# A fused decoder layer on one core: the cross-attention's output product of the first query tile, one slot later

## The chip, the cores and the metric

The kernel runs on one core of a Trainium2 chip. The metric is the device time of the program in microseconds (us): the median of the runs, beside one profiled execution, from which all spans, starts and durations come. Engines are named by what they do here: TensorE (PE in the profile, its weight loads PEld), VectorE (DVE), ScalarE (ACT), GpSimd (POOL) and SyncE (SP, which only issues DMAs here).

## The reference

A post-norm decoder layer over 32 entries of 256 tokens with 256 features, all in float32:

```python
x = _layernorm(x + self_attention(x))             # 16 heads of 64, 4 key/value heads, rotary, alibi
x = _layernorm(x + cross_attention(x, ctx, cell)) # 16 heads of 16, windows of 64 tokens
x = _layernorm(x + ffn(x))                        # 256 -> 1024 gate and up -> 256, quantised
```

The cross-attention normalises its attention output o once more before its output projection:

```python
return _proj(o, ln_o_w, ln_o_b, w_o, b_o)         # _ln(o) @ w_o.T + b_o
```

So for each tile of 128 query tokens: statistics of o, scaling, a product of 256 x 256, the residual, statistics of the sum, scaling. That is the part which the change touches.

## The kernel before, in words

The 256 tokens of an entry are two query tiles (t = 0 and 1) of 128. Everything is a software pipeline written out by hand at the end of `tile_decoder_kernel` (L870 to L945). Time is cut into steps, and each step into two slots (part 0 and part 1); an entry b owns the 16 slots from 16b. Each slot emits the fixed work of self-attention and cross-attention, and then advances the generators that are due in it. A generator (`self_inputs`, `cross_inputs`, `self_output`, `cross_output`, `feed_forward`) emits a piece of work and yields the number of slots until its next piece; a bare `yield` is one slot. TensorE, VectorE and ScalarE keep the order in which the instructions were emitted (L891); GpSimd and SyncE are given theirs by the framework. While entry b + 1 is in self-attention, entry b is in cross-attention and entry b - 1 in its feed-forward, so one slot mixes three entries.

In a slot of part 0 the order is: the inverse of the softmax sums (L433, L435), the exponentials of the second half of a cross unit (`cross_exp`, L684), the generators, then `self_turn` (the transposes t, L447, and their copies pT, L452), `cross_back` (xr, L729, and on VectorE L734 and L735), `cross_turn` (xt, L693, copy xpT, L695), a flush of the scalings that the generators left in the list `last` (L199), `self_scores` (s, L394; VectorE L410; ScalarE's exponentials L420), and every second step `self_values` (o, L464, copy oT, L471). In a slot of part 1 it is: `self_spread` (R, L479), `cross_exp`, the generators, `cross_values` (xo, L709, and its copy xoT, L718), `self_normal` (VectorE, L487), and again a flush.

`cross_output(b, t)` starts in slot 16b + 29 for t = 0 and in slot 16b + 37 for t = 1. Its pieces, one slot apart:
- statistics of o on VectorE (L178, L179) and their inverse root on GpSimd (`rstd_of`, L185 to L187);
- the scaling on ScalarE, through `last`;
- two transposes on TensorE into the bank zoT (L205) and ScalarE's copy to zT (L206);
- the product xw = zT times xo_w (L755, zT is what is loaded as weights), the residual sum on VectorE (L759), its statistics and inverse root (rstd_x);
- the scaling of the sum into x2 (L199).

For t = 0 the product falls into slot 16b + 32, a slot of part 0, and for t = 1 into slot 16b + 40. `feed_forward(b)`, which reads x2 of both tiles, starts in slot 16b + 42. In the slots 16b + 31 to 16b + 34 entry b - 1 is in its feed-forward: the up product (L802, L823), the maxima (L829 to L836), GpSimd's scaling L838 and VectorE's rounding L843. GpSimd also has the rotation of a query (L566 to L568), whose other half comes by two DMAs (L555) behind the eight kTz transfers (L640) on SyncE's queue.

All matmul outputs live in one pool of eight PSUM banks (L88), so a new output waits for the last reader of the bank that it is given. The buffers zT, xoT and x2 are doubled, xpT too.

Of the kernel before, what the change touches and what calls it, by code (L numbers as in the profile page):

```python
# [50 lines left out]
def kernel(  # L51
# [33 lines left out]
    def ctile(shape, dtype, name):  # L85
        return const.tile(shape, dtype, name=name, tag=name)
# [3 lines left out]
    def bank(name, shape=(P, 512), dtype=F32):  # L90
        return ps.tile(list(shape), dtype, tag="b", name=name)
# [12 lines left out]
    def work(name, shape, bufs=2, dtype=F32):  # L104
        return sb.tile(list(shape), dtype, tag=name, name=name, bufs=bufs)
# [50 lines left out]
    for i in range(2):  # L156


        t = ctile([P, (NT + 1) * XH * XE + 32 - XE], F32, f"xvaug{i}")
# [14 lines left out]
    def stats(src, name):  # L174

        st = small("st", 6)
        mv = small(f"mv_{name}", 2)
        nc.vector.bn_stats(st, src)  # L178
        nc.vector.bn_aggr(mv, st)  # L179
        return mv  # L180

    def rstd_of(mv, name):

        rb = small(f"rstd_{name}", 2)
        nc.gpsimd.tensor_scalar(rb[:, 0:1], mv[:, 1:2], EPS, None, ALU.add)  # L185
        nc.gpsimd.tensor_tensor(rb[:, 0:1], rb[:, 0:1], neg_half[:, 0:1], ALU.pow)
        nc.gpsimd.tensor_scalar(rb[:, 1:2], mv[:, 0:1], rb[:, 0:1], -1.0, ALU.mult, ALU.mult)  # L187
        return rb
# [12 lines left out]
    def transposed(dst, src, name):  # L201

        pt = bank(name)
        for dc in range(NDC):
            nc.tensor.transpose(pt[:, dc * P : (dc + 1) * P], src[:, dc * P : (dc + 1) * P], ident)  # L205
        nc.scalar.copy(dst, pt[:, 0 : NDC * P].rearrange("p (c t) -> p c t", t=P))  # L206
# [535 lines left out]
    def cross_output(b, t):  # L742
        s = state[b]
        on = s["on", t]
        mv = stats(on, "zo")
        rstd = rstd_of(mv, "zo")
        yield
        last.append(partial(scaled, on, on, rstd))
        yield
        zoT = work("zT", [P, NDC, P])  # L750
        transposed(zoT, on, "zoT")
        yield
        py = bank("xw")
        for dc in range(NDC):
            nc.tensor.matmul(py[:, 0:D], zoT[:, dc, :], xo_w[:, dc, :], start=(dc == 0), stop=(dc == NDC - 1))  # L755
        if t == 0:
            s["x2"] = work("x2", [P, NT, D])
        h = s["x2"][:, t, :]
        nc.vector.tensor_tensor(h, py[:, 0:D], s["x1", t], ALU.add)  # L759
        mv = stats(h, "x2")  # L760
        rstd = rstd_of(mv, "x2")
        yield
        last.append(partial(scaled, h, h, rstd))
# [117 lines left out]
    for b in range(B):  # L881
        s0 = 16 * b
        if b:
            at(s0 - 16, self_inputs(b))
        at(s0 + 2, cross_inputs(b))
        for t in range(NT):
            at(s0 + 2 * (5 + 4 * t), self_output(b, t))
            at(s0 + 2 * (CROSS + 5 + 4 * t) + 1, cross_output(b, t))
        at(s0 + 2 * (CROSS + 11) + 2, feed_forward(b))
# [145 lines left out]
```

## Time and profile before

| what | value |
|---|---|
| median of 3 runs | 2324.79 us (2323.94 to 2325.04) |
| the profiled execution, its own time | 2327.47 us |
| its span, first to last instruction | 2325.7 us |
| mean granted TensorE clock | 0.987 |
| VectorE / ScalarE / GpSimd busy | 1701.3 / 1764.8 / 1124.2 us |
| steady stretch 250 to 2090 us: TensorE busy | 1827.02 of 1840 us |
| first 250 us: TensorE busy | 227.22 of 250 us |
| from 2090 us on: TensorE busy | 192.68 of 235.7 us |
| one entry, from one first-tile product to the next (913.37 to 983.02) | 69.65 us |

How to read it: a busy share is an average over the span. The ends of TensorE's matmuls are modelled, so the starts of two groups that follow each other tell more than a printed duration. A line in order of time has the start, the duration, engine and line, what is written from what, the shape and the count; in brackets stands how long the engine was idle before it and what ended that.

### The profile page before, as it was taken

The numbers are of one execution on the slowest core, as the hardware profiler recorded it, in microseconds if no ns is written. First come the engines' busy times: TensorE is split into PE (matmuls) and PEld (weight loads), VectorE is DVE, ScalarE is ACT, GpSimd is POOL, SyncE is SP. The second block draws the span as 40 slices with busy tenths as digits, with TensorE's granted clock in tenths as the row PEclk, the third lists the DMA queues.
The fourth block names the chain that finished last, engine by engine and source line by source line (L and its number), as shares of the span: only waits on it lengthen the run. The fifth ranks groups of instructions, "written<-read, shape, count | busy, mean of one in ns | idle before, by whom it ended". The sixth has DMA issues, their size and how long they took to land.

```text
span 2325.7 us, 54754 instructions
## 1 busy us (share of the span) xinstructions
PE 2246.9 (97%) x17637; PEld 1689.2 (73%) x17700; DVE 1701.3 (73%) x6949; ACT 1764.8 (76%) x5057; POOL 1124.2 (48%) x1851
## 2 busy tenths in 40 slices
PE   7999999999999999999999999999999999999985
PEld 5677777777777777777777777777777777777652
DVE  3767777777777777777777777777777777777765
ACT  2677777878777878777878777878777878777873
POOL 5344545445545545545445545445545444545432
PEclk9999999999999999999999999999999999999996
DMA  6311211112211111211111211112211111211000
GB/s 211 87 51 47 58 53 49 47 45 52 59 52 49 47 45 53 57 51 49 47 47 54 56 51 49 47 46 54 56 51 50 46 48 53 55 47 44 20 22 10
DMA packets 105407, 123.05 MB, mean 53 GB/s; under 512 B 21792, under 2 KB 74912, under 8 KB 105120
## 3 DMA queue, kind: packets, MB, share of 16 engines
q1 hardware_dynamic: 103424, 115.96, 18.7%
q10 hardware_dynamic: 1696, 3.57, 0.4%
q8 instruction: 142, 2.33, 0.4%
q14 instruction: 145, 1.19, 0.2%
HBM read 39.50 MB, written 8.39 MB: 21 GB/s over the span
## 4 chain that ended last, share of the span: by engine, by line
PE 78%; DVE 10%; ACT 8%; issue 1%; POOL 1%; DMA 1%; SPq 0%; ACTq 0%; POOLq 0%; DVEq 0%
PE proj L331 12%; PE s L394 10%; PE wo L495 10%; PE t L447 8%; PE o L464 8%; PE xt L693 4%; ACT p L420 4%; PE xs L655 4%; DVE gu L817 3%; PE xw L755 3%; PE xv L616 3%; PE ffo L855 3%; DVE p L410 2%; PE R L479 2%; PE xk L604 2%; PE v L363 2%
## 5 line engine op out<-in xcount | busy, mean ns | idle before, releaser
L420 ACT ACTIVATE p<-p,nm 128x256 f32<-128x256 f32 x1024 | 508.0, 498 | 168.6 <-DVE nm L410 164.7
L410 DVE CUSTOM_DVE_ANT_0 p<-s,alibi 128x256 f32<-128x256 f32 x1024 | 372.7, 420 | 180.5 <-PE s L394 180.4
L452 ACT COPY pT<-t 128x512 f32<-128x512 f32 x512 | 275.2, 591 | 127.1 <-PE t L447 126.8
L684 ACT ACTIVATE xp<-xp,xnm 128x128 f32<-128x128 f32 x1024 | 326.1, 394 | 5.9 <-DVE xnm L668 5.9
L394 PE MATMUL s<-kT,qT 64*128 64x256 f32 x2048 | 290.8, 402 | 0.0
L447 PE MATMUL t<-ident,p 128*128 128x128 f32 x2048 | 269.0, 273 | 3.2 <-ACT p L420 3.2
L447 PEld LDWEIGHTS t<-ident,p 128*128 128x128 f32 x2048 | 237.9, 141 | 31.4 <-ACT p L420 6.6
L331 PE MATMUL proj<-xT,wq_sb 128*128 128x256 f32 x1024 | 251.8, 389 | 0.0
L464 PE MATMUL o<-pT,v 128*64 128x256 f32 x2048 | 250.0, 385 | 0.0
L495 PE MATMUL wo<-wo_sb,oT 128*128 128x256 f32 x1024 | 245.3, 382 | 0.0
L668 DVE CUSTOM_DVE_ANT_0 xp<-xs,mask 128x128 f32<-128x128 f32 x1024 | 225.9, 286 | 2.9 <-PE xs L655 2.1
L495 PEld LDWEIGHTS wo<-wo_sb,oT 128*128 128x128 f32 x1024 | 189.4, 190 | 47.4 <-issue 22.7
L355 POOL TENSOR_TENSOR qT<-qT,other 128x512 f32<-128x512 f32 x128 | 162.9, 1273 | 120.6 <-DMA other<-psin 53.3
L394 PEld LDWEIGHTS s<-kT,qT 64*128 64x128 f32 x2048 | 176.5, 186 | 54.7 <-issue 23.5
L340 DVE TENSOR_TENSOR psin<-proj,rs_sb 128x512 f32<-128x512 f32 x160 | 110.2, 689 | 141.7 <-PE proj L331 141.7
L331 PEld LDWEIGHTS proj<-xT,wq_sb 128*128 128x128 f32 x1024 | 186.4, 191 | 32.8 <-issue 6.4
L464 PEld LDWEIGHTS o<-pT,v 128*64 128x64 f32 x2048 | 135.7, 136 | 98.3 <-issue 22.9
L420 ACT ACTIVATION_READ_ACCUMULATOR p<-p,nm 128x1 f32 x1024 | 192.6, 188 | 0.0
L695 ACT COPY xpT<-xt 128x512 f32<-128x512 f32 x256 | 153.2, 598 | 6.1 <-PE xt L693 4.2
L693 PE MATMUL xt<-ident,xp 128*128 128x128 f32 x1024 | 154.2, 274 | 0.0
L655 PE MATMUL xs<-kTz,xqT 64*64 64x512 f32 (+1 forms) x768 | 136.6, 611 | 5.0 <-POOL xqT L568 5.0
L817 DVE SCALAR_TENSOR_TENSOR gu<-gu,ff 128x512 f32<-128x512 f32 x128 | 82.3, 682 | 72.8 <-ACT gu L816 72.8
(156 smaller groups left out, 4528.2 us busy)
## 6 DMA issues: line engine op xcount, KB each, us to landing
other<-psin SPq DMA_DIRECT2D x640, 64.0 KB, 2.0
xT<-in_xt_dram SPq DMA_DIRECT2D x32, 256.0 KB, 2.7
xs<-in_x_dram SPq DMA_DIRECT2D x32, 256.0 KB, 2.7
cs<-in_ctx_dram SPq DMA_DIRECT2D x32, 256.0 KB, 2.7
other<-qb SPq DMA_DIRECT2D x64, 128.0 KB, 2.0
kTz<-tr SPq DMA_DIRECT2D x256, 32.0 KB, 2.0
other<-qb SPq DMA_DIRECT2D x128, 64.0 KB, 1.9
out_dram<-x SPq DMA_DIRECT2D x32, 256.0 KB, 2.2
```

Of the source, the lines that this page charges most:

```text
L331: nc.tensor.matmul(pq[:, c * L : (c + 1) * L], w[:, dc, c * P : (c + 1) * P], xT[:, dc, :], start=(dc == 0), stop=(dc == NDC - 1),)
L394: nc.tensor.matmul(banks[half][:, rr * L : (rr + 1) * L], qT[rows_, rr, qc * P : (qc + 1) * P], kT[rows_, kc, :], start=(rr == 0), stop=(r ...
L410: nc.vector.tensor_tensor_reduce(p[:, cols], banks[half][:, cols], alibi[:, 2 * (4 * kc + 2 * rp + rr) + half, :], -0.125, 3.0e38, ALU.add ...
L420: nc.scalar.activation(p[:, cols], p[:, cols], AF.Exp, bias=nm[:, rr : rr + 1], scale=-1.0, accum_out=s["sums", i // 2][:, (2 * rp + rr) * ...
L447: nc.tensor.transpose(pt[:, j * P : (j + 1) * P], p[half][:, rr * L + kk * P : rr * L + (kk + 1) * P], ident,)
L452: nc.scalar.copy(pT[half], pt)
L464: nc.tensor.matmul(po[half * HD : (half + 1) * HD, rp * L : (rp + 1) * L], s["v"][:, kk, (2 * kc + half) * HD : (2 * kc + half + 1) * HD], ...
L495: nc.tensor.matmul(py[:, 0:D], s["oT", qc, kc][:, r, :], wo_sb[:, 4 * kc + r, :], start=(kc == 0 and r == 0), stop=(kc == 1 and r == 3),)
L655: nc.tensor.matmul(banks[half].rearrange("p (h k) -> p h k", k=P)[q0:q1], s["xqT", qc][rows_, ch, q0:q1], kTz[rows_, ch, :, k0 : k0 + P], ...
L668: nc.vector.tensor_tensor_reduce(p[:, cols], banks[half][:, cols], s["mask"][:, qc, :], -1.0, 3.0e38, ALU.add, ALU.min, s["xnm", i][half][ ...
L684: nc.scalar.activation(p[:, cols], p[:, cols], AF.Exp, bias=s["xnm", i][half][:, j : j + 1], scale=-1.0)
L693: nc.tensor.transpose(pt[:, j * P : (j + 1) * P], p[:, j * P : (j + 1) * P], ident)
```

## The change

One yield in `cross_output` now counts two slots for the first query tile, and one as before for the second:

```diff
         zoT = work("zT", [P, NDC, P])
         transposed(zoT, on, "zoT")
-        yield
+        yield 1 + (t == 0)
         py = bank("xw")
         for dc in range(NDC):
             nc.tensor.matmul(py[:, 0:D], zoT[:, dc, :], xo_w[:, dc, :], start=(dc == 0), stop=(dc == NDC - 1))
```

So for t = 0 the product and all behind it (the sum, its statistics, the inverse root, the scaling) come one slot later: the product in slot 16b + 33 and the scaling in slot 16b + 34. On TensorE the product then stands behind t, xr, xt, s, o and R, and ahead of wo (L495). On VectorE L759, L178 and L179 stand behind the four score operations L410 and behind L836, ahead of L487. On GpSimd rstd_x stands behind the rotation L566 to L568, in most entries between the two L838. On ScalarE the scaling stands behind the copies pT and xpT of the next slot and ahead of its exponentials. The PSUM banks are handed out in the new order, so t, xr, xt, s, o, R and wo of that stretch get other banks than before. No operation is added or taken away, and no DMA is moved.

## The prediction

> **What bounds the kernel now.** I read the page's busy rows and slices first, then the chain that ended last, then TensorE's waits (cut to the steady stretch, 250 to 2090 us), then one entry's turn in order of time, engine by engine.
>
> ```profile
> PE 2246.9 (97%) x17637; PEld 1689.2 (73%) x17700; DVE 1701.3 (73%) x6949; ACT 1764.8 (76%) x5057; POOL 1124.2 (48%) x1851
> PEclk9999999999999999999999999999999999999996
> PE 78%; DVE 10%; ACT 8%; issue 1%; POOL 1%; DMA 1%; SPq 0%; ACTq 0%; POOLq 0%; DVEq 0%
> ```
>
> TensorE is busy for 97% of the span at full clock and carries 78% of the chain. So only what TensorE waits for, or what its stream contains, is worth anything. Its waits in the steady stretch are a single line (columns: who waited, for whom; us in total, times, longest):
>
> ```profile
> PE xw L755 <- ACT zT L206: 10.2, 26, 0.4
> ```
>
> That is the product this change moves, waiting for ScalarE's copy of the transposed tile. Over the whole run it is 17.4 us in 34 waits: 31 are the first query tile of entries 0 to 30, three belong to the drain at the end. The second tile's product never waits in the steady state. One entry (TensorE, then ScalarE, in order of time; start, duration, then the group):
>
> ```profile
> 911.94 1.04 PE L802 MATMUL ff<-ff_up,xiT 128*128 128x512 bf16 x3
> 913.37 1.13 PE L755 MATMUL xw<-xo_w,zT 128*128 128x256 f32 x4 [0.40 <-ACT zT L206]
> 914.34 1.04 PE L447 MATMUL t<-ident,p 128*128 128x128 f32 x8
> 915.21 0.38 PE L729 MATMUL xr<-ident,xoT 128*128 128x128 f32 x2
> ```
>
> ```profile
> 912.97 0.35 ACT L206 COPY zT<-zoT 128x256 f32<-128x256 f32 x1
> 913.22 0.37 ACT L718 COPY xoT<-xo 128x256 f32<-128x256 f32 x1
> 913.48 1.29 ACT L684 ACTIVATE xp<-xp,xnm 128x128 f32<-128x128 f32 x4
> 915.03 1.07 ACT L452 COPY pT<-t 128x512 f32<-128x512 f32 x2 [0.26 <-PE t L447]
> ```
>
> The same product for the second tile, where nothing is late, gives the undisturbed pace:
>
> ```profile
> 947.13 1.03 PE L755 MATMUL xw<-xo_w,zT 128*128 128x256 f32 x4
> 947.99 1.04 PE L447 MATMUL t<-ident,p 128*128 128x128 f32 x8
> 948.87 0.38 PE L729 MATMUL xr<-ident,xoT 128*128 128x128 f32 x2
> ```
>
> **What the stall really costs.** The 0.40 us shown is counted from a modelled matmul end, so I use starts. Undisturbed, the four records of the product take 947.99 - 947.13 = 0.86 us, and the eight transposes 0.88 us. The four records of the feed-forward group (one is missing) also take 0.86, so the product was due at 911.94 + 0.86 = 912.80 and came at 913.37: 0.57 late. It then took 914.34 - 913.37 = 0.97 instead of 0.86, because its own weights (zT is the stationary operand) could not be loaded ahead: another 0.11. The stall is 0.68 us per entry.
>
> **What is late next.** With the product gone from this place, the transposes t start at 912.80; their exponentials were finished at 911.39 (ScalarE's order of time), and the PSUM banks that the changed program gives them were read last by VectorE at 911.85 and by ScalarE's bias at 913.06 (needed by the second group's weight load at about 913.13: just in time). The transposes end at 912.80 + 0.88 = 913.68, and next is xr, whose weights are xoT. ScalarE writes that right after zT: 913.22 + 0.37 = 913.59, plus the 0.05 that passed between zT's end (913.32) and the product (913.37) = 913.64, plus 0.11 for a weight load that wasn't ahead = 913.75. So a small wait of about 0.07 remains. In before, xr came at 915.21; less the 0.86 of product that moves behind it, 914.35. Gain per entry: 914.35 - 913.75 = **0.60 us**. The bounds: 0.68 if xoT makes no wait, and nothing if a later wait eats it all.
>
> **Parts that cost nothing, and their cover.**
> The product itself: the same four records, in the next slot between R and wo. Its bank was freed by a copy of pT some 2 us earlier and zT has been ready for over 4 us; TensorE pays 0.86 there as it did here.
> VectorE: the sum and statistics (L759, L178, L179: 0.42 + 0.43 + 0.18, about 1.0 us) leave the queue ahead of xr's normalisation and the self scores, where VectorE had 0.79 us of idleness waiting for s, and enter behind the feed-forward's L836, ahead of L487. L836 ended at 920.54 and would end near 919.1 (the scores start 0.60 + 0.86 = 1.46 us earlier); the product, behind R, is done at about 919.0; L487 then ends near 920.9, and VectorE stood waiting until 921.68 anyway for GpSimd (the lines are GpSimd's, VectorE's and ScalarE's):
>
> ```profile
> 920.52 1.13 POOL L838 TENSOR_SCALAR gu<-gu,ffhup 128x1024 f32<-128x1024 f32 x1
> 921.68 0.69 DVE L843 TENSOR_SCALAR gu<-gu 128x1024 bf16<-128x1024 f32 x1 [0.54 <-POOL gu L838]
> 924.75 0.51 ACT L420 ACTIVATE p<-p,nm 128x256 f32<-128x256 f32 x1 [1.37 <-DVE nm L410]
> ```
>
> So 0.8 us of cover. If it were gone, L487, L843 and the next scores behind L759 would be late.
> GpSimd: rstd_x (0.22 + 0.57 + 0.27, with gaps 1.26 us) moves from ahead of the rotation L566 to 568 behind the first L838. L566 started at 918.28 on a DMA that SyncE issued only after eight kTz transfers, so the rotation, the first L838 and L843 stay where they are in time. The second L838 waits for VectorE until 924.29, behind which 1.26 us fit.
> ScalarE: the scaling L199 (0.60) moves into the next slot, ahead of four exponentials. They wait 1.37 us for VectorE there; rstd_x comes at 922.9 to 923.5, so L199 ends by 924.1. It hides, with 0.6 to spare. SyncE's queue keeps its order; the change issues no DMA.
> Semaphore waits: the first t now waits for three engines, which needs one or two more wait instructions of 0.051 us on TensorE's sequencer, at most 0.1 x 31 = 3 us. The t of the next slot already has two waits and starts on its pace; I take zero.
>
> **A rule that speaks against it.** L843 used to start with GpSimd idle; now rstd_x stands ready behind L838. The Trainium skill (SBUF — State Buffer, "Who interferes with whom") says that GpSimd and a VectorE copy or tensor_scalar in a two-port mode take one pair of ports in turn, each for its whole instruction. One place of this trace has just that, with another GpSimd operation queued behind L838:
>
> ```profile
> 2238.50 1.20 DVE L843 TENSOR_SCALAR gu<-gu 128x1024 bf16<-128x1024 f32 x1 [0.19 <-POOL gu L838]
> 2238.43 0.73 POOL L566 TENSOR_TENSOR qb<-qb,rx_sb 128x256 f32<-128x256 f32 x1
> 2239.12 1.18 POOL L567 TENSOR_TENSOR other<-other,rx_sb 128x256 f32<-128x256 f32 x1
> ```
>
> L843 lost 0.51 (1.20 against 0.69) to the one operation that was ahead, and then went before the next. By that row L843 loses what is left of the first rstd operation, 0.15 to 0.22 us. By the rule read at its worst (all three first) it loses 1.26. What follows L843 is VectorE's chain to the scores, ScalarE's exponentials (924.75) and at last the copies of pT, which TensorE's group o needs. Those copies ran from 930.23 to 931.30 against a need, after the 0.60 shift, at 931.89 - 0.60 + 0.70 = 931.99: 0.64 us of slack, with 0.05 for the semaphore. A delay of 0.2 costs nothing; 1.26 costs 0.62 per entry and with it the gain.
>
> **Sum.** 31 entries x 0.60 = 18.6 us. The last entry's product does not wait (its ScalarE is ahead), and in the drain the move shifts about 1 us of VectorE work by a slot: taken as zero, within 0.5 either way. The profiled execution took 2327.47 us (span 2325.7): it would be 2308.9. The median of the runs is 2324.79, 2.7 below that execution: **2306.2**.
>
> **Rivals.**
> 1. Part of the gain is eaten. L843 loses two GpSimd operations (0.22 + 0.57 + a gap of 0.08 = 0.87): 0.87 - 0.64 = 0.23 per entry at o, 7 us: 2313. Or ScalarE's xoT comes 0.3 later than now: 9 us, 2315. For it: ScalarE is in one run from 904 to 913 with hardly a gap. Against it: the offsets of zT and xoT to the product are the same within 0.01 us in all 31 entries. Chance 0.20.
> 2. The wait merely moves to xr, xt or o, so that the kernel doesn't do what the move says: 2324. That would need ScalarE to be the bound from slot to slot, but it waited 0.26 for t at 915.03 and 0.94 for the scores after that. Chance 0.05.
> 3. Slower: rstd_x becomes late and, at the head of ScalarE's queue, L199 holds back the exponentials behind it. It decides from 1.24 us of delay of these (0.64 slack + 0.60 gain), which is rstd_x at 925.4, 2 us after my estimate. At 925.75 it costs 0.31 x 31 = 10 us: 2334. Against it: the rotation ahead of it is held by the SyncE queue to a fixed time. Chance 0.05.
>
> **How the numbers follow.** The main case is 2303.8 (0.68 per entry) to 2309.5 (0.1 per entry for waits and semaphores): 0.68; a little more gain 0.02. The range goes on to 2314 to take in the first half of rival 1. A measurement of this kernel tells 0.2% (4.6 us) from no change, so everything below 2320.1 is faster: 0.68 + 0.02 + 0.20 = 0.90; the same 0.05; slower 0.05.
>
> **What would show it.** After: no wait of xw on zT in the steady stretch; t following the feed-forward's group at once; xr with a wait of 0.0 to 0.1 us on xoT; the period of an entry 69.65 (913.37 to 983.02) less 0.60; the scores' first VectorE operation 1.5 us earlier relative to the feed-forward; L843 at 0.7 to 0.9 us, and L199 of the first tile between xpT and the exponentials with no wait behind it. I'd be wrong if TensorE shows a new wait of over 0.3 us at xr or at o, or if ScalarE's exponentials of the next slot wait for L199.

## The result and the profile after

| kernel | median us | runs | range |
|---|---|---|---|
| before | 2324.91 | 6 | 2323.94 to 2326.14 |
| changed | 2305.03 | 6 | 2303.58 to 2307.11 |

The ratio is 0.9916, with a 95% interval of 0.9903 to 0.9928: 19.9 us less. The forecast was 2306.2. The profiled execution of the changed kernel took 2305.13 us, its span 2303.3.

The same rows of the page as were shown of before, now of the changed kernel:

```profile
PE 2244.9 (97%) x17700; PEld 1692.6 (73%) x17700; DVE 1697.7 (74%) x6949; ACT 1757.6 (76%) x5057; POOL 1137.0 (49%) x1851
PE 93%; DVE 3%; ACT 2%; POOL 1%; DMA 1%; issue 1%; SPq 0%; POOLq 0%; DVEq 0%; ACTq 0%
```

TensorE's busy time is what it was (2246.9 before); the span shrank around it. The chain that ended last now lies on TensorE for 93% instead of 78%: it no longer leaves TensorE for VectorE and ScalarE once an entry in order to reach zT. In the steady stretch the table of TensorE's waits is empty. The busy time of the same 1820 us (stretch, its length, then TensorE's busy time and records, granted clock, DMA share, GB/s), of before:

```profile
250.00:2070.00 1820.00, 1807.07 (x14364) 1.00 0.19 51
```

and of the changed kernel:

```profile
250.00:2070.00 1820.00, 1820.00 (x14538) 1.00 0.20 51
```

By the modelled ends of its matmuls TensorE has not one gap left there. One entry of the changed kernel on TensorE, in order of time:

```profile
905.66 1.04 PE L802 MATMUL ff<-ff_up,xiT 128*128 128x512 bf16 x4
906.54 1.04 PE L447 MATMUL t<-ident,p 128*128 128x128 f32 x8
907.41 0.39 PE L729 MATMUL xr<-ident,xoT 128*128 128x128 f32 x2
907.64 0.60 PE L693 MATMUL xt<-ident,xp 128*128 128x128 f32 x4
...
911.11 0.66 PE L479 MATMUL R<-ident,wide 128*128 128x128 f32 x4
911.60 1.03 PE L755 MATMUL xw<-xo_w,zT 128*128 128x256 f32 x4
912.47 1.89 PE L495 MATMUL wo<-wo_sb,oT 128*128 128x256 f32 x8
```

and the two copies on ScalarE that it used to wait for:

```profile
906.68 0.36 ACT L206 COPY zT<-zoT 128x256 f32<-128x256 f32 x1
906.94 0.37 ACT L718 COPY xoT<-xo 128x256 f32<-128x256 f32 x1
```

The transposes t follow the feed-forward's group at once (0.88 us from start to start), xr follows t after 0.87, and the product, now 4.56 us behind the end of zT, takes 912.47 - 911.60 = 0.87. The next entry's product starts at 980.61, so an entry takes 980.61 - 911.60 = 69.01 us. Before it took 69.65. That is 0.64 to 0.65 us an entry, and 31 x 0.65 = 20 us, the whole difference.

### The profile page after: what moved, and what is told of

Same layout as the page of the kernel before. It is cut to its first block, busy times and chain, and to the rows that moved or that the text cites. A ratio compares the mean times of both kernels' runs of the same rounds, so it can differ in the third digit from the quotient of the medians.

```text
span 2303.3 us, 54792 instructions
## 1 busy us (share of the span) xinstructions
PE 2244.9 (97%) x17700; PEld 1692.6 (73%) x17700; DVE 1697.7 (74%) x6949; ACT 1757.6 (76%) x5057; POOL 1137.0 (49%) x1851
## 4 chain that ended last, share of the span: by engine, by line
PE 93%; DVE 3%; ACT 2%; POOL 1%; DMA 1%; issue 1%; SPq 0%; POOLq 0%; DVEq 0%; ACTq 0%
PE proj L331 12%; PE s L394 11%; PE o L464 10%; PE wo L495 9%; PE t L447 9%; PE xs L655 5%; PE ff L802 5%; PE xt L693 5%; PE R L479 3%; PE xo L709 3%; PE xv L616 3%; PE ffo L855 3%; PE xw L755 2%; PE xq L532 2%; PE xk L604 2%; PE v L363 2%
## 5 line engine op out<-in xcount | busy, mean ns | idle before, releaser
L410 DVE CUSTOM_DVE_ANT_0 p<-s,alibi 128x256 f32<-128x256 f32 x1024 | 372.5, 420 | 161.6 <-PE s L394 161.2
L495 PE MATMUL wo<-wo_sb,oT 128*128 128x256 f32 x1024 | 245.2, 382 | 0.0
L495 PEld LDWEIGHTS wo<-wo_sb,oT 128*128 128x128 f32 x1024 | 191.8, 190 | 49.0 <-issue 23.5
L566 POOL TENSOR_TENSOR qb<-qb,rx_sb 128x256 f32<-128x256 f32 (+1 forms) x96 | 87.6, 913 | 125.7 <-DMA other<-qb 76.5
```

The lines of the kernel that those rows point to most:

```text
L410: nc.vector.tensor_tensor_reduce(p[:, cols], banks[half][:, cols], alibi[:, 2 * (4 * kc + 2 * rp + rr) + half, :], -0.125, 3.0e38, ALU.add ...
L495: nc.tensor.matmul(py[:, 0:D], s["oT", qc, kc][:, r, :], wo_sb[:, 4 * kc + r, :], start=(kc == 0 and r == 0), stop=(kc == 1 and r == 3),)
```

## The experiments

Each ratio is to the kernel before, run on the same chip, with its 95% interval. A period is the mean time from one entry's key projection (L604) to the next one's, over 25 entries, from the starts in the trace; it is 69.66 us before and 69.00 in the changed kernel.

| run | median us | ratio to before | period us |
|---|---|---|---|
| product in its old slot, a ready operand | 2306.34 | 0.9919 [0.9905, 0.9933] | 69.00 |
| product in its old slot, the rest a slot later | 2325.13 | 1.0002 [0.9993, 1.001] | 69.65 |
| product two slots later | 2332.72 | 1.0033 [1.002, 1.0045] | 69.82 |
| changed, one ScalarE step ahead of xoT | 2307.15 | 0.9922 [0.991, 0.9935] | 69.09 |
| changed, only the scaling a slot later | 2306.29 | 0.9923 [0.9911, 0.9935] | 69.02 |
| changed, more VectorE work ahead of the scores | 2312.29 | 0.9946 [0.9934, 0.9959] | 69.20 |
| changed, two GpSimd powers more | 2305.29 | 0.9918 [0.9905, 0.9932] | 69.01 |
| changed, four GpSimd powers more | 2307.87 | 0.9927 [0.9914, 0.9941] | 69.03 |
| changed, five ScalarE steps ahead of xoT | 2319.03 | 0.9976 [0.9966, 0.9986] | 69.47 |
| changed, a chain of eight GpSimd additions | 2323.16 | 0.9991 [0.9983, 0.9999] | 69.42 |

### The wait alone, without the move

```diff
+            lhs = zoT[:, dc, :] if t else xo_w[:, dc, 0:P]
-            nc.tensor.matmul(py[:, 0:D], zoT[:, dc, :], xo_w[:, dc, :], start=(dc == 0), stop=(dc == NDC - 1))
+            nc.tensor.matmul(py[:, 0:D], lhs, xo_w[:, dc, :], start=(dc == 0), stop=(dc == NDC - 1))
```

> The kernel before, with its order kept: the product of the first query tile stays in its slot, but takes a block of the weights xo_w as its stationary operand in place of zT, so it has nothing to wait for (zT is still made, and not read; the cross-attention's output of the first tile is therefore something else). Theory (the gain is the wait on zT and nothing else): TensorE's wait at L755 is gone in the steady stretch, 0.66 us an entry, x 31 = 20.5, so 2304 to 2305, as fast as the changed kernel. Rival (the gain comes of the new order on VectorE, ScalarE and the PSUM banks, the wait only being where it showed): most of it stays away, 2315 to 2325, and a wait shows at the next product or transposes.

Measured: 2306.34, and the period of the changed kernel to the hundredth. The order of the kernel before costs nothing by itself; its wait on zT is the whole of the 20 us. The rival, a gain through the new order, is out.

### Everything but the product moved

```diff
             nc.tensor.matmul(py[:, 0:D], zoT[:, dc, :], xo_w[:, dc, :], start=(dc == 0), stop=(dc == NDC - 1))
+        if t == 0:
+            yield
```

> The kernel before with the product in its old slot, but all behind it (the sum and its statistics on VectorE, the inverse root on GpSimd, the scaling on ScalarE) one slot later, as in the changed kernel. Theory: the wait on zT stays, 2324 to 2326, although VectorE's scores start earlier. Rival (the gain is VectorE's and ScalarE's new order): 2305 to 2312.

Measured: 2325.13, no change. TensorE's waits of this run in the stretch from 250 to 2070 us (who waited, for whom; us, times, longest):

```profile
PE xw L755 <- ACT zT L206: 10.1, 26, 0.4
```

The row is that of before within 0.1 us. VectorE's earlier scores bring nothing as long as TensorE stands still.

### The product two slots later

```diff
-        yield 1 + (t == 0)
+        yield 1 + 2 * (t == 0)
```

> The changed kernel with the first tile's product two slots later than before in place of one, ahead of the transposes of the next step. Theory: any place works where zT is ready and the sum is in time for the feed-forward: 2304 to 2306, TensorE without a wait at the product. Rival (the place one slot later is special, because the work behind the product hides there): VectorE's sum now stands ahead of the scores of a slot whose exponentials follow VectorE at once, so 2310 or more.

Measured: 2332.72, slower than before the change: my theory as it stood there fell. TensorE's order is that of the changed kernel, group by group (R, xw, wo, t), because no fixed TensorE work stands between these two places. What moved is VectorE's sum and statistics, and ScalarE's scaling. In order of time, TensorE of this run:

```profile
918.13 1.03 PE L755 MATMUL xw<-xo_w,zT 128*128 128x256 f32 x4
919.00 1.89 PE L495 MATMUL wo<-wo_sb,oT 128*128 128x256 f32 x8
...
930.43 1.13 PE L394 MATMUL s<-kT,qT 64*128 64x256 f32 x8
932.10 2.47 PE L464 MATMUL o<-pT,v 128*64 128x256 f32 x16 [0.54 <-ACT hiT L851]
934.50 0.66 PE L479 MATMUL R<-ident,wide 128*128 128x128 f32 x4
```

VectorE's, where the sum stands directly ahead of the scores of the next step:

```profile
924.48 0.41 DVE L759 TENSOR_TENSOR x<-xw,x 128x256 f32<-128x256 f32 x1
924.92 0.43 DVE L178 BATCH_NORM_STATS2 st<-x 128x6 f32<-128x256 f32 x1
925.38 0.18 DVE L179 BATCH_NORM_AGGREGATE mv_x<-st 128x2 f32<-128x6 f32 x1
925.48 0.39 DVE L410 CUSTOM_DVE_ANT_0 p<-s,alibi 128x256 f32<-128x256 f32 x1
```

and, of SyncE, TensorE and ScalarE, the eight kTz transfers, the scores two slots ahead of o and the copy hiT:

```profile
909.68 6.13 SPq L640 DMA_DIRECT2D kTz<-tr  x8
922.13 1.13 PE L394 MATMUL s<-kT,qT 64*128 64x256 f32 x8
931.06 0.99 ACT L851 COPY hiT<-hiT 128x1024 bf16<-128x1024 bf16 x1
```

The same three of the changed kernel:

```profile
903.15 5.75 SPq L640 DMA_DIRECT2D kTz<-tr  x8
915.60 1.13 PE L394 MATMUL s<-kT,qT 64*128 64x256 f32 x8
922.66 0.99 ACT L851 COPY hiT<-hiT 128x1024 bf16<-128x1024 bf16 x1
```

The product doesn't wait, but o does. Undisturbed, o follows s after 1.06 us and R follows o after 1.88 (909.23 - 908.17 and 911.11 - 909.23 in the changed kernel). Here it is 1.67 and 2.40, so in this entry o lost 0.61 + 0.52 = 1.13 us: first, by the releaser that the line names, to ScalarE's copy hiT, then to the copies pT behind it. ScalarE's copy hiT started 931.06 - 922.13 = 8.93 us after the start of s two slots earlier. In the changed kernel it was 922.66 - 915.60 = 7.06. So ScalarE came 1.87 us late and TensorE lost 1.13: a slack of 0.74 us. VectorE's 1.0 us and the scaling's 0.5, now between xoT and the exponentials of the second half, explain 1.5 of the 1.87. The rest came by SyncE's queue: the eight kTz transfers, whose issue began 12.45 us ahead of s in both, kept it for 6.13 us here and for 5.75 there, and the DMAs L555 behind them, GpSimd's rotation L566, its scaling L838 and VectorE's L843 all came 0.4 later behind them.

This start differs from entry to entry; why SyncE's queue takes longer in one than in another stays open. Over 25 entries of this run TensorE lost 0.12 to 2.08 us, 0.82 in the mean by the period. Read over 25 entries each of the changed kernel and of the runs built on it, o loses nothing as long as hiT starts no more than 7.79 us behind s, and about the excess from there on (0.04 us at 7.83, 0.11 at 7.90, 0.19 at 7.98). For the entry shown of the changed kernel that is a slack of 7.79 - 7.06 = 0.73 us. In its other entries hiT starts 6.42 to 7.72 us behind s, so the slack lies between 0.07 and 1.37. The entry with the least of it (GpSimd, TensorE, ScalarE):

```profile
1326.30 0.73 POOL L566 TENSOR_TENSOR qb<-qb,rx_sb 128x256 f32<-128x256 f32 x1 [2.75 <-DMA other<-qb]
1329.61 1.14 PE L394 MATMUL s<-kT,qT 64*128 64x256 f32 x8
1337.33 0.99 ACT L851 COPY hiT<-hiT 128x1024 bf16<-128x1024 bf16 x1
```

### How close xr stands

```diff
+        if i == 2:
+            nc.scalar.copy(small("step", 1), neg_half[:, 0:1])
         nc.scalar.copy(oT, po[:, 0 : 2 * P])
```

> The changed kernel with one more small ScalarE copy (128 x 1, some 0.2 us with its start) in front of the copy to xoT in the slot ahead of the transposes xr, once an entry. Theory (after the change TensorE reaches xr with no slack: xoT's end sets it within 0.05 us): each 0.2 us shows in full, 31 x 0.2 = 6 us, 2311, with a wait at xr on xoT. Rival (there is slack at xr): 2305.

Measured: 2307.15, 2.1 us more than the changed kernel and not 6; by the intervals alone that is not clear of none. The periods tell more: 0.09 us an entry. The step's record lasts 0.20 us, but xoT started only 0.10 after it: I had taken the record's length for the price, although the Trainium skill (ScalarE: Activation LUTs, "What ACT_TABLE_LOAD costs") says that activations one behind the other overlap by some 93 ns, which fits 0.20 - 0.10 here, where the operations are copies. Five steps make the dose clear:

```diff
         if i == 2:
-            nc.scalar.copy(small("step", 1), neg_half[:, 0:1])
+            for _ in range(5):
+                nc.scalar.copy(small("step", 1), neg_half[:, 0:1])
```

> The changed kernel with five small ScalarE copies in front of the copy to xoT in place of one. One of them moved xoT by 0.10 us (from start to start), so five move it by 0.5. Theory (TensorE reaches xr with no slack, and a wait there costs its length): xr comes 0.5 to 0.6 us later in each entry, 16 to 19 us, 2321 to 2324, so nearly the whole gain is gone and the wait stands at xr on xoT. Rival (ScalarE takes it up, since it waits for TensorE at the next copies anyway): under 2312.

Measured: 2319.03, 14 us of the 20 given back. ScalarE of that run:

```profile
910.99 0.56 ACT L720 COPY step<-neg_half 128x1 f32<-128x1 f32 x5
911.45 0.37 ACT L721 COPY xoT<-xo 128x256 f32<-128x256 f32 x1
```

TensorE:

```profile
910.59 1.04 PE L447 MATMUL t<-ident,p 128*128 128x128 f32 x8
911.87 0.44 PE L732 MATMUL xr<-ident,xoT 128*128 128x128 f32 x2 [0.25 <-ACT xoT L721]
912.15 0.60 PE L693 MATMUL xt<-ident,xp 128*128 128x128 f32 x4
```

xoT moved by 911.45 - 910.99 = 0.46 us and the period by 69.47 - 69.00 = 0.47: one for one, a little under the 0.5 to 0.6 expected. There is no slack at xr; the changed kernel arrives there just when xoT does.

### The scaling's place, and VectorE's

```diff
         rstd = rstd_of(mv, "x2")
-        yield
+        yield 1 + (t == 0)
         last.append(partial(scaled, h, h, rstd))
```

> The changed kernel with only ScalarE's scaling L199 of the first tile one more slot later, so that it stands behind xoT and ahead of the second half's exponentials, as it does in the run with the product two slots later. It puts 0.5 us into ScalarE's stretch ahead of the copies hiT and pT, which TensorE's group o waits for. In the run two slots later that stretch came 1.87 us later relative to TensorE than in the changed kernel and o waited 1.13, so the slack is 0.74 us. Theory (one stretch with 0.74 us of slack): 0.5 is hidden, 2304 to 2306. Rival (the scaling's new place is what cost the time there): 0.5 x 31 = 15 us, 2320.

Measured: 2306.29, period 69.02. The 0.5 us on ScalarE are hidden, as the slack says, but for four of 25 entries whose slack was smaller than that: they lost 0.04 to 0.27 us.

```diff
         yield
+        if t == 0:
+            for _ in range(3):
+                nc.vector.bn_stats(small("more", 6), wo_sb[:, 0, :])
         last.append(partial(scaled, h, h, rstd))
```

> The changed kernel with three more VectorE statistics of a constant (0.45 us each from start to start, 1.35 in all) once an entry, right ahead of the scores two slots behind the product's old place; nothing reads them. Theory: 1.35 less 0.74 of slack shows at o, 0.61 x 31 = 19 us, 2324. Rival (VectorE's place doesn't matter, ScalarE's does): 2305.

Measured: 2312.29, 7 us more and not 19. The dose was smaller than I had reckoned: from VectorE's order of time of this run,

```profile
920.70 1.07 DVE L765 BATCH_NORM_STATS2 more<-wo_sb 128x6 f32<-128x256 f32 x3
921.68 0.41 DVE L410 CUSTOM_DVE_ANT_0 p<-s,alibi 128x256 f32<-128x256 f32 x1
```

the three took 0.98 us together (they depend on nothing, and run 0.33 apart), and hiT came 926.78 - 918.82 = 7.96 us after s, 0.90 late. TensorE at o in this entry:

```profile
928.18 2.11 PE L464 MATMUL o<-pT,v 128*64 128x256 f32 x16
930.23 0.65 PE L479 MATMUL R<-ident,wide 128*128 128x128 f32 x4
```

o took 2.05 instead of 1.88, a loss of 0.17, so the slack is again 0.73. Over 25 entries the loss ran from nothing to 0.89 us, and the period grew by 0.20. The mechanism held, and the size of the dose was wrong.

### A late inverse root

```diff
         mv = stats(h, "x2")
+        if t == 0:
+            late = small("late", 1)
+            for _ in range(2):
+                nc.gpsimd.tensor_tensor(late, mv[:, 1:2], neg_half[:, 0:1], ALU.pow)
```

> The changed kernel with two more GpSimd powers (0.57 us each, 1.3 with their gaps) ahead of the first tile's inverse root, once an entry; nothing reads them. The inverse root is then ready 1.3 us later, ScalarE's scaling L199 waits for it, and the exponentials behind L199, which had 0.64 us to spare, start some 0.6 later. Theory (0.74 us of slack at o): nothing of it shows, 2304 to 2307. Rival (the third one of the prediction: a late inverse root at the head of ScalarE's queue decides): 0.6 x 31 = 19 us, 2324.

Measured: 2305.29. GpSimd and ScalarE of this run:

```profile
908.89 0.73 POOL L566 TENSOR_TENSOR qb<-qb,rx_sb 128x256 f32<-128x256 f32 x1 [2.71 <-ACT p L420]
915.32 0.51 ACT L420 ACTIVATE p<-p,nm 128x256 f32<-128x256 f32 x1
```

The first exponential of the slot started 3.08 us after s (915.32 - 912.24) against 2.47 (918.07 - 915.60) in the changed kernel, 0.61 late. That looks like the expectation, but it is not the powers' doing: GpSimd's rotation L566 was itself 0.61 later against s in this entry, and the exponential came 915.32 - 908.89 = 6.43 us behind L566, just as in the changed kernel (918.07 - 911.64). The powers made only the scaling L199 later, which started 914.76 - 912.24 = 2.52 us after s instead of 1.24, 0.67 of it by them; the 0.64 us of idle time ahead of the exponentials took that up. So this dose never got as far as o, and its time says nothing on the slack there.

> The same with four more powers, 2.6 us. The exponentials start some 1.9 us later. Theory: 1.9 less 0.74 shows at o, 1.15 x 31 = 36 us, 2341. Rival (the stretch has more slack, because the scaling is not on the path to o): under 2315.

Measured: 2307.87, not 2341. The dose didn't arrive: nothing orders these powers against the inverse root, so GpSimd's queue got them mixed, one even behind it, and the exponentials came only 917.77 - 914.89 = 2.88 us after s, 0.41 late. In this entry the run says nothing against 0.7 us of slack, and nothing for it. So the delay was made a chain:

```diff
         mv = stats(h, "x2")
+        if t == 0:
+            for _ in range(8):
+                nc.gpsimd.tensor_scalar(mv[:, 1:2], mv[:, 1:2], 0.0, None, ALU.add)
```

> The changed kernel with eight GpSimd additions of 0.0 to the first tile's variance, one behind the other, ahead of its inverse root, so that none of them can be put beside it (some 0.3 us each, 2.4 to 2.7 in all). The inverse root is late by that; less the 0.64 us that the exponentials had to spare, they start 1.8 to 2.1 later. Theory (0.70 to 0.74 us of slack at o): 1.1 to 1.4 us at o in each entry, 34 to 43 us, 2339 to 2348, slower than before the change, with a wait at o on the copies hiT and pT. Rival (the path to o is not through the scaling): 2305 to 2312.

Measured: 2323.16, 18 us of the 20 gone, but not slower than before. GpSimd of that run:

```profile
917.53 1.12 POOL L841 TENSOR_SCALAR gu<-gu,ffhup 128x1024 f32<-128x1024 f32 x1
918.61 2.59 POOL L763 TENSOR_SCALAR mv_x<-mv_x 128x1 f32<-128x1 f32 x8
921.28 0.21 POOL L185 TENSOR_SCALAR rstd_x<-mv_x 128x1 f32<-128x1 f32 x1
```

ScalarE:

```profile
922.55 0.60 ACT L199 ACTIVATE x<-x,rstd_x 128x256 f32<-128x256 f32 x1 [2.39 <-POOL rstd_x L187]
923.05 0.49 ACT L420 ACTIVATE p<-p,nm 128x256 f32<-128x256 f32 x1
```

TensorE:

```profile
919.30 1.13 PE L394 MATMUL s<-kT,qT 64*128 64x256 f32 x8
...
928.67 2.47 PE L464 MATMUL o<-pT,v 128*64 128x256 f32 x16
931.07 0.66 PE L479 MATMUL R<-ident,wide 128*128 128x128 f32 x4
```

L199 came 922.55 - 919.30 = 3.25 us after s instead of 916.84 - 915.60 = 1.24: 2.01 late. The exponentials were 3.75 - 2.47 = 1.28 late, and o took 2.40 instead of 1.88, 0.52 longer. Slack at o: 1.28 - 0.52 = 0.76. So the path from the inverse root over ScalarE's queue to o is real. It took 2 us of delay to use up most of the gain in this entry, since there are two slacks one behind the other, 2.01 - 1.28 = 0.73 ahead of the exponentials and 0.76 at o. Not all entries lose as much: over 25 of them the loss runs from 0.01 to 1.23 us, with the start of L566, and the mean period grew by 0.42. The median lost a few us more than 31 x 0.42 = 13. Of the 16.8 us by which the span grew (2320.1 against 2303.3), 4.0 lie behind the last entry's key projection, in the drain of the pipeline; what holds it up there stays open.

## Why the prediction was right

**The stall.** It was put at 0.68 us an entry, and the kernel with a ready operand in the old order gained 0.66 of period. That the wait is the whole cause is shown by that run and by the one that moved all but the product.

**What is late next.** The prediction saw a wait of 0.07 at xr, worked out with 0.11 for a weight load that isn't ahead, and so a gain of 0.60. xr came 907.41 - 906.54 = 0.87 after t, on the pace: the gain is 0.65, and this term was the one mis-sized. xoT ended at 907.31, and a matmul that follows its weights by so little lost nothing to be seen. That it would be xr, and that it stands on the edge, was right: five steps on ScalarE came back one for one. 31 x 0.05 = 1.6 us is the distance from 2306.2 to 2305.0, within a few tenths.

**Work that moved at no cost.** On VectorE, L759 started at 912.67 without a wait, L487 at 913.69, and L843 still stood 0.66 us for GpSimd's L838. The cover was there. GpSimd's inverse root did meet L843, with its first operation alone, but the other way round than the prediction had it. Of the changed kernel, GpSimd:

```profile
913.85 1.12 POOL L838 TENSOR_SCALAR gu<-gu,ffhup 128x1024 f32<-128x1024 f32 x1
915.05 0.73 POOL L185 TENSOR_SCALAR rstd_x<-mv_x 128x1 f32<-128x1 f32 x1
915.87 0.57 POOL L186 TENSOR_TENSOR rstd_x<-rstd_x,neg_half 128x1 f32<-128x1 f32 x1
```

VectorE:

```profile
915.00 0.69 DVE L843 TENSOR_SCALAR gu<-gu 128x1024 bf16<-128x1024 f32 x1 [0.66 <-POOL gu L838]
```

and ScalarE:

```profile
916.84 0.60 ACT L199 ACTIVATE x<-x,rstd_x 128x256 f32<-128x256 f32 x1 [0.39 <-POOL rstd_x L187]
918.07 0.51 ACT L420 ACTIVATE p<-p,nm 128x256 f32<-128x256 f32 x1 [0.64 <-DVE nm L410]
```

L843 started 0.05 us ahead of GpSimd's L185 and lost nothing (0.69 as before); L185 took 0.73 instead of 0.22, and by the trace it did so in all 29 entries from the second to the last but two (for the second tiles, with no L843 beside them, 0.21 to 0.23). L185 ended at 915.78, just behind the end of L843 at 915.69. That fits what the Trainium skill (SBUF — State Buffer, "Who interferes with whom") says, that whoever issues first holds the shared ports for its whole instruction, but VectorE was first here. The price, 0.51 us on GpSimd, made L199 wait 0.39, where the prediction had no wait; the exponentials behind it still had their 0.64 to spare. The end effect was right, and the loser was not.

**The slack at o.** Predicted 0.64 in the entry that it works out; three runs give 0.74, 0.73 and 0.76 in that entry. The agreement is in part luck, for two terms were off in opposite directions. The prediction had o need its second copy pT by 0.65 us behind its own start. In the changed kernel that copy ends 1.95 us behind the start of hiT (923.55 + 1.06 - 922.66) and o starts 924.96 - 915.60 = 9.36 us behind s, so the loss, which sets in at 7.79, says 7.79 + 1.95 - 9.36 = 0.38. That takes 0.27 off the 0.64. And the rotation did not stay where it was in time: L566 came 3.96 us ahead of s, where it would have been 922.53 - 0.60 - 918.28 = 3.65, had it stayed while s came 0.60 earlier. That gave 0.31 back. The prediction called the rotation "held by the SyncE queue to a fixed time" and took one slack for all entries. Against TensorE it is not held: in 25 entries of the changed kernel L566 started 4.59 to 3.31 us ahead of s. None of these entries lost more than 0.01 us at o, but one of them had only 0.07 left. That the gain came whole is to this extent luck too.

**The rivals.** The first, a part of the gain eaten at xr or o, didn't happen, but both of its places are real: 0.46 us at xr cost 14 us, and 2 us on GpSimd cost 18. The second, the wait only moving on, is refuted by the period, which fell by 0.65, and by the starts of xr, o and R, which kept their pace in 25 entries. The empty table of waits alone would not do: it is empty in the run with more VectorE work too, where the period grew by 0.20, because a wait inside the group o doesn't show in it. The third, a late inverse root, is a real path, and its turning point, 2 us later than the estimate, is about where the chain of additions puts it: 2.0 us later cost 18 us of the 20, though it came unevenly, entry by entry. A place that made the kernel slower was found elsewhere: one slot more for VectorE's sum.

## What to carry to other kernels

Where one engine is the bound, read its waits in the steady stretch alone, and price a stall by starts against the same group where nothing is late: 0.68 us here, where the page's idle time said 0.40 and the run without the wait gave 0.66. The starts also show a wait inside a group, which the table of waits leaves out. Give a waiting group time by putting ready work ahead of it, but then follow everything behind the moved group on the other engines, because TensorE's order may be the same in a place that gains 20 us and in one that loses 8. And measure the slack left over by doses, with operations that depend on each other, reading from the trace whether the dose arrived, and in more than one entry: here the slack ranged from 0.07 to 1.37 us with the start of one DMA, and in a single entry that looked like the effect of a dose.

## What the hardware showed that I had not expected

- Small operations overlap: a ScalarE copy of 128 x 1 has a record of 0.20 us, but cost 0.09 to 0.10 from start to start. Independent VectorE statistics of 128 x 256 ran 0.33 us apart with records of 0.41 to 0.42.
- Of two instructions released by the same end of a GpSimd operation, VectorE's, which waited on its semaphore, started 0.05 us ahead of GpSimd's own next one (and GpSimd lost its 0.51 us in all 29 entries); in the drain of the kernel before it had been the other way round (L566 ahead of L843 by 0.07).
- TensorE's granted clock stayed at 1.00 for 1820 us without a gap in its records.
- The lead of GpSimd's rotation over the scores behind it differs by 1.28 us between the entries of one execution, while TensorE's period stays within 0.01 us.
